# A cross-attention kernel on one core: moving casts, loads and evacuations between slots, and reordering its fill and its end

## The chip, the cores and the metric

The kernel runs on one core of a Trainium2 chip. The metric is the device time of one execution in microseconds (us), as the median of several runs. A core has a matrix engine (TensorE, PE in the profile; PEld is its weight load), a vector engine (VectorE, DVE), a scalar engine (ScalarE, ACT), a general engine (GpSimd, POOL) and a queue that only issues DMAs (SyncE, SP). Each engine works through its own instructions in program order, and waits on semaphores for the others. TensorE writes its products to PSUM; all else is in SBUF or in DRAM.

## The reference: what is computed

The inputs are x (32 batches of 512 rows of 640), a context (32 batches of 77 rows of 1024) and weights. All is float32.

```python
q = _heads(hidden_states @ to_q_w)                       # 20 heads of 32
h_txt = _sdpa(q, _heads(ehs_txt @ to_k_w), _heads(ehs_txt @ to_v_w))
...
out = out @ to_out_w + to_out_b
out = (out + residual) / RESCALE
```

`_sdpa` is softmax(q k^T / sqrt(32)) v. The context has exactly 77 rows, so the three other attentions of the reference work on empty slices, and their weights are not used. The output is attention, the output projection, its bias and x itself added.

## The kernel before

**Arithmetic.** Float32 operands are split in two float32r parts, a high part (a cast) and a low part (the source minus the high part), and a product is three matmuls: high by high, high by low, low by high (`PAIRS`, L127). So nearly every tile costs a cast, usually on ACT, and a subtraction on DVE or GpSimd.

**Order.** The order of the instructions of each engine is the program's (`manual_schedule`, L267): what the Python code calls first stands first on the engine, and DMAs on their queue. A tile pool hands out buffers (`bufs`), and a tile that takes a used buffer waits for the readers of the old one.

**First phase: keys and values.** Keys and values of all batches are computed in five groups of up to 512 context rows (L294 to L383), split (`split_keys` L207, `split_values` L222) and stored in DRAM (`k_dram`, `v_dram`). Query weights are loaded and split beside that, output weights too; these go to `wo_dram` (`split_wo`, L318). The values of the last group are left for the first slots of the next phase (`beside`).

**Second phase: slots.** A slot is one batch and one chunk of four heads: n = 5 b + j, 160 in all. "First" to "fifth slot" below are j = 0 to 4. In slot n (`slot`, L701) TensorE computes the scores of n in four blocks of 128 query rows (`scores` L464, each with a maximum per row on DVE, L486), the queries of slot n + 1 (`queries` L437), the product of probabilities and values of slot n - 4 (`values` L566), and a quarter of the output projection of an earlier batch (`piece` L637, matmuls L622). ACT computes exponentials (`exps` L491), GpSimd normalises (`normalize` L509), DVE transposes (`transpose_p` L517), and the probabilities go to DRAM (`pd`, SP) and come back transposed as a tile `raw` (`load_p` L533, two loads). There `cast_p` (L540) casts the last 64 rows (L544) and the rest (L545), `last_p` (GpSimd, L558) and `rest_p` (DVE, L551) make the low parts. `PASSES` (L564) gives the order in which the values' matmuls use them: first the cast, then the rows with `last_p`'s part, then `rest_p`'s.

After `values`, `copy_a` (ACT) and `add_a` (DVE) add the two halves; a slot later `high_a` (ACT, L599) and `low_a` (DVE, L604) make the operands of the output projection. `finish` (L648) evacuates closed projection banks with the residual added (DVE, L654) and stores them; there are two banks `po`. `split_q` (L451) copies the queries: ACT, two copies on GpSimd (L458), two subtractions on DVE (L460).

**Special slots.** A slot is "filling" when n > 0 and there is no finished batch to project yet (n = 1 to 7). In filling slots the big cast is GpSimd's. Values begin with slot 4 (`takes`, L665). `end` (L845) works off the last four slots' probabilities and the last projections.

**Queues.** SP issues nearly all DMAs: keys and values of a batch (`refill` L686), `pd` stores, `raw` loads, x, residuals, outputs. Each issue takes SP's time too, so what stands ahead on SP counts.

Lines that the steps below touch: L213, L234, L376, L544, L545, L551, L558, L599, L604, L654, L717 to L722, L754, L759, L783, L829 to L833, L845 to L887, L937 to L945.

## Time and profile before

| | us |
|---|---|
| median of 3 runs | 1945.45 (1943.25 to 1946.92) |
| the profiled execution's own time | 1956.04 |
| its span, first to last instruction | 1954.3 |
| PE, DVE, ACT, POOL busy | 1902.4, 1638.7, 1532.9, 1376.5 |
| first scores start (end of the first phase) | 265.0 |
| last scores' maximum (slot 159) | 1906.1 |

The profile is of one execution that is 10.6 us longer than the median run; sums made from its rows are made against 1956.04. A row of the timeline gives start, length, engine, line, operation, tiles and form; in brackets stand the engine's idle time before it and what ended that. A row of waits gives total, number of times and the longest. "x4" means that four instructions of one kind are drawn together. A matmul's busy time is modelled, since matmuls overlap; short waits inside a group show only as a longer group.

### The profile page before, as it was taken

The numbers are of one execution on the slowest core, as the hardware profiler recorded it, in microseconds if no ns is written. First come the engines' busy times: TensorE is split into PE (matmuls) and PEld (weight loads), VectorE is DVE, ScalarE is ACT, GpSimd is POOL, SyncE is SP. The second block draws the span as 40 slices with busy tenths as digits, with TensorE's granted clock in tenths as the row PEclk, the third lists the DMA queues.
The fourth block names the chain that finished last, engine by engine and source line by source line (L and its number), as shares of the span: only waits on it lengthen the run. The fifth ranks groups of instructions, "written<-read, shape, count | busy, mean of one in ns | idle before, by whom it ended". The sixth has DMA issues, their size and how long they took to land.

```text
span 1954.3 us, 37691 instructions
## 1 busy us (share of the span) xinstructions
PE 1902.4 (97%) x10332; PEld 1663.2 (85%) x10332; DVE 1638.7 (84%) x2494; ACT 1532.9 (78%) x6206; POOL 1376.5 (70%) x1264
## 2 busy tenths in 40 slices
PE   9999997999999999999999999999999999999998
PEld 7888886888888888888888888888888888888887
DVE  4444447899999989989999999999999999999995
ACT  3232247888899889888888888989988889889883
POOL 1000057888888888878888787888888888788874
PEclk9999998999999999999999999999999999999999
DMA  9878868898898988888888888988889898888875
GB/s 188 197 190 251 190 184 207 216 232 227 227 237 227 223 227 225 228 219 231 223 235 226 227 225 227 235 231 232 221 234 229 229 229 225 227 223 228 230 201 168
DMA packets 570657, 431.39 MB, mean 221 GB/s; under 512 B 199440, under 2 KB 479120, under 8 KB 570448
## 3 DMA queue, kind: packets, MB, share of 16 engines
q1 hardware_dynamic: 566832, 416.36, 84.6%
q0 software_dynamic: 3520, 12.45, 1.8%
q8 instruction: 86, 1.41, 0.3%
q14 instruction: 123, 1.01, 0.2%
q10 hardware_dynamic: 96, 0.16, 0.0%
HBM read 247.17 MB, written 181.64 MB: 219 GB/s over the span
## 4 chain that ended last, share of the span: by engine, by line
PE 43%; POOL 15%; DMA 13%; DVE 9%; ACT 7%; issue 7%; SPq 5%; POOLq 0%; DVEq 0%; ACTq 0%
PE po L622 11%; PE pq L443 11%; DMA raw<-pd 8%; PE pk L191 7%; PE pv L191 7%; POOL pn L513 5%; PE pa L573 4%; PE sc L478 4%; ACT pn L496 3%; POOL pp L558 3%; POOL qt L458 3%; POOL xt L264 2%; DMA xs<-in_x_dram 2%; DVE nm L486 2%; DVE pp L551 2%
## 5 line engine op out<-in xcount | busy, mean ns | idle before, releaser
L496 ACT ACTIVATE pn<-sc,nm 128x77 f32<-128x77 f32 x2560 | 794.3, 331 | 58.0 <-DVE nm L486 53.1
L622 PE MATMUL po<-wo_s,at 128*128 128x320 f32 x3840 | 629.1, 312 | 17.9 <-DVE xr L654 13.2
L443 PE MATMUL pq<-xt,wq_s 128*128 128x512 f32 x2400 | 631.5, 403 | 1.2
L622 PEld LDWEIGHTS po<-wo_s,at 128*128 128x128 f32 x3840 | 575.6, 188 | 47.8 <-DVE xr L654 26.5
L496 ACT ACTIVATION_READ_ACCUMULATOR pn<-sc,nm 128x1 f32 x2560 | 539.1, 211 | 0.0
L513 POOL TENSOR_TENSOR pn<-pn,rs 128x616 f32<-128x616 f32 x320 | 448.4, 1419 | 116.4 <-DVE rs L506 105.2
L443 PEld LDWEIGHTS pq<-xt,wq_s 128*128 128x128 f32 x2400 | 429.7, 191 | 85.8 <-POOL xt L264 10.8
L478 PEld LDWEIGHTS sc<-kb,qt 128*128 128x128 f32 x1920 | 327.2, 189 | 63.6 <-POOL qt L458 11.8
L478 PE MATMUL sc<-kb,qt 128*128 128x154 f32 (+1 forms) x1920 | 317.5, 273 | 16.4 <-POOL qt L458 7.7
L573 PE MATMUL pa<-pp,vb 128*128 128x512 f32 x960 | 295.7, 412 | 9.1 <-issue 5.1
L486 DVE TENSOR_REDUCE nm<-sc 128x4 f32<-128x308 f32 x640 | 285.6, 457 | 14.1 <-PE sc L478 9.3
L458 POOL CAST qt<-qt 64x512 fp32r<-64x512 f32 x320 | 194.9, 609 | 132.7 <-ACT qt L454 93.3
L551 DVE TENSOR_TENSOR pp<-raw,pp 128x1024 fp32r<-128x1024 f32 x160 | 272.3, 1702 | 14.2 <-ACT pp L545 11.9
L520 DVE STREAM_TRANSPOSE z<-pn 128x1280 f32<-128x1280 f32 x160 | 241.8, 1512 | 35.5 <-POOL pn L513 28.0
L558 POOL TENSOR_TENSOR pp<-raw,pp 64x512 fp32r<-64x512 f32 x160 | 207.0, 1294 | 56.8 <-ACT pp L544 44.6
L588 DVE TENSOR_TENSOR pa<-pa,aw 64x512 f32<-64x512 f32 x320 | 222.6, 696 | 14.6 <-ACT aw L583 4.1
L264 POOL TENSOR_TENSOR xt<-xs,xt 128x512 fp32r<-128x512 f32 x160 | 202.8, 1294 | 36.4 <-ACT xt L263 33.4
L460 DVE TENSOR_TENSOR qt<-pq,qt 64x512 fp32r<-64x512 f32 x320 | 218.6, 683 | 10.0 <-ACT qt L454 5.0
L615 POOL TENSOR_TENSOR xr<-xr,bias 128x640 f32<-128x640 f32 x128 | 203.2, 1588 | 12.4 <-PE sc L478 3.0
L573 PEld LDWEIGHTS pa<-pp,vb 128*128 128x128 f32 x960 | 160.3, 190 | 46.5 <-POOL pp L558 15.8
L544 ACT CAST pp<-raw 64x512 fp32r<-64x512 f32 x160 | 99.2, 620 | 101.2 <-DMA raw<-pd 97.4
L583 ACT COPY aw<-pa 64x1024 f32<-64x1024 f32 x160 | 162.0, 1013 | 19.2 <-PE pa L573 15.5
(47 smaller groups left out, 1656.5 us busy)
## 6 DMA issues: line engine op xcount, KB each, us to landing
pd<-z SPq DMA_DIRECT2D x640, 160.0 KB, 3.4
raw<-pd SPq DMA_DIRECT2D x160, 512.0 KB, 4.4
xr<-in_x_dram SPq DMA_DIRECT2D x128, 320.0 KB, 3.8
out_dram<-xr SPq DMA_DIRECT2D x127, 320.0 KB, 3.7
xs<-in_x_dram SPq DMA_DIRECT2D x124, 320.0 KB, 7.2
raw<-pd SPq DMA_DIRECT2D x160, 128.0 KB, 4.4
v_dram<-vs SPq DMA_DIRECT2D x80, 192.0 KB, 4.0
k_dram<-ks POOLq DMA_DIRECT2D x20, 512.0 KB, 4.7
```

Source lines behind the costliest of these rows:

```text
L191: nc.tensor.matmul(held[j][:, :gn], w[:, k, a, :], cts[g, k][:, c, :gn], start=(k == 0 and n == 0), stop=(k == NK - 1 and n == 2),)
L264: low.tensor_tensor(parts[1], src, parts[0].bitcast(F32), ALU.subtract)
L443: nc.tensor.matmul(pqs[n], wq_s[:, k, a, j * P : (j + 1) * P], xts[b, k][:, c, :], start=(k == 0 and m == 0), stop=(k == NC_ - 1 and m == 2),)
L458: nc.gpsimd.tensor_copy(qt[other, 1 + w, :], qt[r, 0, :].bitcast(F32))
L478: nc.tensor.matmul(sc[:, cols], qt[:, m, t * P : (t + 1) * P], keys_, start=(m == 0), stop=(m == 2),)
L486: nc.vector.tensor_reduce(nm, sc[:, :KCOLS].rearrange("p (h k) -> p h k", k=NKEY), AX.X, ALU.max, negate=True)
L496: nc.scalar.activation(pnb[n % 2][:, at, :NKEY], sc[:, i * NKEY : (i + 1) * NKEY], AF.Exp, bias=nm[:, i : i + 1], accum_out=sms[n][:, at : ...
L513: nc.gpsimd.tensor_tensor(pf, pf, rs[:, k : k + half].unsqueeze(2).to_broadcast([P, half, NKEY]), ALU.mult)
L551: nc.vector.tensor_tensor(pp[:, 2:4, :], raw[:, 0:2, :], pp[:, 0:2, :].bitcast(F32), ALU.subtract)
L558: nc.gpsimd.tensor_tensor(pp[64:, 4, :], raw[:64, 2, :], pp[:64, 4, :].bitcast(F32), ALU.subtract)
L573: nc.tensor.matmul(pas[n][:, p, :], vb[:, p, t, :], pp[:, c, :], start=(c == p), stop=(c == p + 2),)
L622: nc.tensor.matmul(pos[b, t, h][:, :HALF], ats[b * NC_ + j][:, a, t * P : (t + 1) * P], wos[0][:, j, c, h * HALF : (h + 1) * HALF], start= ...
```

## The change

It does these things.

- **Fourth slot.** `cast_p` is parted: `cast_rows` casts the last 64 rows. Third slots cast the rows of the tile that the fourth slot takes, before their last exponentials. From the fourth slot on (j >= 3) `high_a` goes before the big cast; so far only j = 4 did that.
- **Loads of probabilities** go at the top of the slot in third slots and in filling slots (`soon`), instead of after the second scores.
- **Fifth slot.** `finish()` is called before the last scores too.
- **Filling slots.** The big cast comes after the second exponentials, `rest_p` before and `last_p` and the key copies after `split_q`. Exponentials of the fourth block go ahead of `copy_a` and x splits, and of the value splits beside.
- **Output weights** are loaded once, into the tiles of z, the second value tile and the bias before these are needed, and split in slots 1, 2 and 5. `wo_dram` goes.
- **Values beside** (last group, chunks 2 to 4): the low part and the four stores move from DVE and SP to GpSimd.
- **First slot.** The last group's last two key stores are issued by ACT. Both key loads, the output weights and x of batch 1 follow on SP; x of batch 1 was on GpSimd's queue. The second value tile is zeroed in slot 3.
- **End.** The load for slot 158 moves ahead of the residual, the eight value loads and the last transpose; one `finish()` goes.

TensorE's order of matmuls is the same in both.

```diff
-    wo_dram = dram.tile([P, NC_, 2, C], FPR, name="wo_dram")
...
-    def split(hi, lo, src):
+    def split(hi, lo, src, low=nc.vector):
         nc.scalar.copy(hi, src)
-        nc.vector.tensor_tensor(lo, src, hi.bitcast(F32), ALU.subtract)
+        low.tensor_tensor(lo, src, hi.bitcast(F32), ALU.subtract)
...
         split(ks[:, 0, :gn], ks[:, 1, :gn], pks.pop(j)[:, :gn])
-        engine = nc.gpsimd if g + 1 < len(GROUPS_KV) else nc.sync
+        engine = nc.gpsimd if g + 1 < len(GROUPS_KV) else nc.sync if j < 3 else nc.scalar
         j0 = GROUPS[GROUP_OF[j]][0]
...
-    def split_values(g, j, between=None):
+    def split_values(g, j, between=None, low=nc.vector):
...
             between()
-        split(vs[:, :na, 0], vs[:, :na, 2], vt)
+        split(vs[:, :na, 0], vs[:, :na, 2], vt, low)
+        queue = nc.sync if low is nc.vector else low
         dst = v_dram[g0 : g0 + gn, :, j].rearrange("(a t) i c d -> i t a (c d)", t=Q)
         for i in range(HPC):
-            nc.sync.dma_start(
+            queue.dma_start(
                 dst[i].bitcast(F32),
...
         nc.gpsimd.tensor_copy(kb[64:, 3], kb[64:, 2].bitcast(F32))
+
+    def zero_values(g):
+        vbs[g] = main.tile([P, GROUPS[g][1], 2, 2, P], FPR, tag=f"vb{g}", name=f"vb{g}")
+        nc.gpsimd.memset(vbs[g].bitcast(F32), 0.0)
...
+    def cast_rows(n):
+        pps[n] = late[0].tile([P, 5, S], FPR, tag="pp", name="pp", bufs=1)
+        nc.scalar.copy(pps[n][:64, 4, :], raws[n][:64, 2, :])
+
     def cast_p(n, shared=False):
...
         raw = raws[n]
-        pp = late[0].tile([P, 5, S], FPR, tag="pp", name="pp", bufs=1)
-        nc.scalar.copy(pp[:64, 4, :], raw[:64, 2, :])
-        (nc.gpsimd.tensor_copy if shared else nc.scalar.copy)(pp[:, 0:2, :], raw[:, 0:2, :])
-        pps[n] = pp
+        if n not in pps:
+            cast_rows(n)
+        (nc.gpsimd.tensor_copy if shared else nc.scalar.copy)(pps[n][:, 0:2, :], raw[:, 0:2, :])
...
-        raw, pp = raws.pop(n), pps[n]
+        raw, pp = raws[n], pps[n]
         nc.vector.tensor_tensor(
...
-    WO = {1: (0, 1, 2), 5: (3,), 6: (4,)}
+    WO = {1: (0, 1), 2: (2, 3), 5: (4,)}
     wos = []
+    wo_raw = {}
+
+    def load_wo(tag, *ks):
+        rows = wo.rearrange("(c p) n -> p c n", p=P)
+        raw = main.tile([P, len(ks), C], F32, tag=tag, name="wo_raw")
+        for i, k in enumerate(ks):
+            nc.sync.dma_start(raw[:, i], rows[:, k])
+            wo_raw[k] = raw[:, i]
+
+    def split_wo(k):
+        split(wos[0][:, k, 0], wos[0][:, k, 1], wo_raw[k])
...
                 load_x(b + 1, (3,))
-            load_keys(b, 1, heads)
+            if b:
+                load_keys(b, 1, heads)
         elif j == 1 and b:
...
         filling = n > 0 and not has_out
+        soon = n >= LATE and (filling or j == 2)
+        if soon:
+            load_p(n - LAG + 1)
         if not filling:
...
             copied = None
-        if taken is not None and j != NC_ - 1:
-            cast_p(taken, filling)
+        if taken is not None and not filling and j < 3:
+            cast_p(taken)
         if n - 1 in takes:
             high_a(takes[n - 1])
-        if taken is not None and j == NC_ - 1:
-            cast_p(taken, filling)
+        if taken is not None and not filling and j >= 3:
+            cast_p(taken)
         bias_now = j in BIAS and b >= BIAS[j][0]
...
             normalize(n - 1, rss.pop(n - 1))
-        if taken is not None:
+        if taken is not None and not filling:
             last_p(taken)
-        if copied is not None:
+        if copied is not None and not (filling and taken is not None):
             copy_keys(copied)
...
             low_a(takes[n - 1])
-        if taken is not None:
+        if taken is not None and not filling:
             rest_p(taken)
-        if n == LATE + 2:
-            nc.sync.dma_start(bias, bo.unsqueeze(0).to_broadcast([P, C]))
-        if n >= LATE:
+        if n == LATE + 3:
+            biases.append(main.tile([P, C], F32, tag="bias", name="bias"))
+            nc.sync.dma_start(biases[0], bo.unsqueeze(0).to_broadcast([P, C]))
+        if n >= LATE and not soon:
             load_p(n - LAG + 1)
...
             refill(b, j, 0)
-        for k in WO.get(n, ()):
-            nc.sync.dma_start(wos[0][:, k].bitcast(F32), wo_dram[:, k].bitcast(F32))
         refill(b, j, 1)
...
         exps(n, 1, *s)
+        if taken is not None and filling:
+            cast_p(taken, True)
+        for k in WO.get(n, ()):
+            split_wo(k)
+        if n == 3:
+            load_wo("bias", 4)
+            zero_values(1)
         for i in turns[0]:
...
                 values(taken, 0, 4)
+                finish()
                 s3 = scores(n, 3)
...
         if ahead:
+            if taken is not None and filling:
+                rest_p(taken)
             split_q(n + 1)
+            if taken is not None and filling:
+                last_p(taken)
+                if copied is not None:
+                    copy_keys(copied)
             if parted:
...
                 values(taken)
-        if len(beside) > 0:
-            context_values(LAST, beside[0], psv)
+        for c in beside:
+            values_of(LAST, c, psv)
         finish()
...
             transpose_x(b + 1, i)
-        if taken is not None:
+        if has_out:
             copy_a(taken)
-        for c in xsplits[1]:
-            split_x(b + 1, c)
+            for c in xsplits[1]:
+                split_x(b + 1, c)
+            if j == 2:
+                cast_rows(takes[n + 1])
         exps(n, 3, *s)
+        for c in beside:
+            split_values(LAST, c, low=nc.gpsimd)
+        if not has_out:
+            if taken is not None:
+                copy_a(taken)
+            for c in xsplits[1]:
+                split_x(b + 1, c)
         if has_out and j in (4, 0, 1):
...
             add_a(taken)
-        if len(beside) > 1:
-            context_values(LAST, beside[1], psv)
         if has_out:
...
         load_p(N - 3)
-        load_values(last, 1)
-        load_residual(last - 1, 3)
         piece(last - 1, 4)
...
         rest_p(N - 4)
+        load_p(N - 2)
+        load_residual(last - 1, 3)
+        load_values(last, 1)
         transpose_p(N - 1)
         add_bias(last - 1, 2)
-        load_p(N - 2)
         piece(last - 1, 5)
...
         steps(last - 1, 32, 37)
-        finish()
         values(N - 3)
...
     load_keys(0, 0)
+    load_keys(0, 1)
+    load_wo("z", 0, 1)
+    load_wo("vb1", 2)
+    load_wo("bias", 3)
+    load_x(1)
     queries(0, 0, NC_)
...
     copy_keys(0)
-    for vb in vbs:
-        nc.gpsimd.memset(vb.bitcast(F32), 0.0)
+    zero_values(0)
     context_values(LAST, 0, psv)
```

The hunks left out drop the loads and splits of the output weights from the first phase, and arguments that nothing uses any more.

More of the change, by code (lines that the diff above doesn't have):

```diff
@@ L99, with load_weights @@
     v_dram = dram.tile([NT + KPAD - NKEY, HPC, NC_, 3, HD], FPR, name="v_dram")
-    wo_dram = dram.tile([P, NC_, 2, C], FPR, name="wo_dram")
-    def split(hi, lo, src):
+    def split(hi, lo, src, low=nc.vector):
         nc.scalar.copy(hi, src)
-        nc.vector.tensor_tensor(lo, src, hi.bitcast(F32), ALU.subtract)
-    def load_weights(w, k0, kn, permuted=True, queues=(nc.sync,) * 4, tag="wraw"):
+        low.tensor_tensor(lo, src, hi.bitcast(F32), ALU.subtract)
+    def load_weights(w, k0, kn, queues=(nc.sync,) * 4, tag="wraw"):
         raw = kvw.tile([P, 2, C], F32, tag=tag, name="wraw", bufs=3 if tag == "wraw" else 2)
-        if permuted:
-            rows = w.rearrange("(q c i) n -> q i c n", q=4, i=Q)
-            for q, queue in enumerate(queues):
-                queue.dma_start(raw[q * Q : (q + 1) * Q, :kn], rows[q, :, k0 : k0 + kn])
-        else:
-            rows = w.rearrange("(c p) n -> p c n", p=P)
-            nc.sync.dma_start(raw[:, :kn], rows[:, k0 : k0 + kn])
+        rows = w.rearrange("(q c i) n -> q i c n", q=4, i=Q)
+        for q, queue in enumerate(queues):
+            queue.dma_start(raw[q * Q : (q + 1) * Q, :kn], rows[q, :, k0 : k0 + kn])
         for k in range(kn):
@@ L243, with load_x @@
     xts, xss, xpool = {}, {}, []
-    def load_x(b, quarters=range(4), queue=nc.sync):
+    def load_x(b, quarters=range(4)):
         if b not in xss:
@@ L251, in load_x @@
         for q in quarters:
-            queue.dma_start(xs[q * Q : (q + 1) * Q, :, :], src[q])
+            nc.sync.dma_start(xs[q * Q : (q + 1) * Q, :, :], src[q])
     def transpose_x(b, i):
@@ L316, in split_wq @@
         split_weights(wq_s[:, k], wq, k, scale=SCALE)
-    def split_wo():
-        k = len(split_ks) - NC_
-        split_ks.append(k)
-        ws = kvw.tile([P, 2, C], FPR, tag="ws", name="ws", bufs=2)
-        split_weights(ws, wo, k)
-        nc.sync.dma_start(wo_dram[:, k].bitcast(F32), ws.bitcast(F32))
     load_context(1, NK)
@@ L348 @@
                     split_keys(0, 4)
-                split_values(g, 3, (None, split_wq, split_wo, None)[g])
+                split_values(g, 3, (None, split_wq, None, None)[g])
                 context(g + 1, *range(3, NK))
@@ L359 @@
                     load_x(0)
-            split_values(g, j, (None, split_wq, split_wo, None)[g])
+            split_values(g, j, (None, split_wq, None, None)[g])
         if g + 1 < LAST:
             load_context(g + 2, NK)
-            if g < 2:
+            if not g:
                 for k in range(0, NC_, 2):
-                    load_weights((wq, wo)[g], k, min(2, NC_ - k), permuted=g == 0)
+                    load_weights(wq, k, min(2, NC_ - k))
             for k in range(NK):
@@ L375 @@
         split_x(0, c)
-    load_x(1, queue=nc.gpsimd)
     for round_ in (range(3), range(3, NC_)):
@@ L393 @@
     raws, pps, ats, pds, sms, pqs, pas, xrs, pos, aws, rss = ({} for _ in range(11))
-    bias = main.tile([P, C], F32, name="bias")
+    biases, zs = [], []
     kbs, vbs, pnb = [], [], []
@@ L405 @@
     qts = [main.tile([P, 3, S], FPR, name=f"qt{n}") for n in range(2)]
-    z = main.tile([P, NBLK, NQ, Q], F32, name="z")
     for g, (j0, nj) in enumerate(GROUPS):
-        vb = main.tile([P, nj, 2, 2, P], FPR, name=f"vb{g}")
-        vbs.append(vb)
+        vbs.append(None)
     def load_keys(b, g, heads=range(HPC)):
@@ L517, in transpose_p @@
     def transpose_p(n):
-        pn = pnb[n % 2]
+        if not zs:
+            zs.append(main.tile([P, NBLK, NQ, Q], F32, tag="z", name="z"))
+        z, pn = zs[0], pnb[n % 2]
         nc.vector.transpose(
@@ L614, in add_bias @@
     def add_bias(b, t):
-        nc.gpsimd.tensor_tensor(xrs[b, t], xrs[b, t], bias, ALU.add)
+        nc.gpsimd.tensor_tensor(xrs[b, t], xrs[b, t], biases[0], ALU.add)
     def output_bank(b, t, h):
```

## The prediction

> **What bounds the kernel now.** I read the page's busy shares and slices first, then stretches of the span, then the waits, then the timeline of one batch.
>
> ```profile
> PE 1902.4 (97%) x10332; PEld 1663.2 (85%) x10332; DVE 1638.7 (84%) x2494; ACT 1532.9 (78%) x6206; POOL 1376.5 (70%) x1264
> ...
> PE   9999997999999999999999999999999999999998
> ```
>
> TensorE (PE) is busy in every slice but the seventh and the last, so at most the 52 us that it idles can go, plus waits too short to show as gaps. The stretches show where they are (PE busy is the first figure behind the length, PEclk the granted clock, then the DMA engines' share):
>
> ```profile
> 318.00:350.00 32.00, 25.04 (x105) 19.83 (x104) 27.30 (x42) 23.17 (x103) 23.82 (x22) 0.87 1.00 234
> ...
> 361.00:1898.00 1537.00, 1515.37 (x8541) 1334.05 (x8540) 1418.86 (x2155) 1366.22 (x5692) 1250.88 (x1136) 1.00 0.88 227
> ...
> 1926.00:1930.00 4.00, 0.00 (x0) 0.00 (x0) 0.71 (x2) 2.15 (x3) 1.26 (x1) 1.00 0.91 265
> ...
> 316.00:319.40 3.40, 3.19 (x8) 2.50 (x9) 2.70 (x5) 0.77 (x2) 1.63 (x3) 0.50 1.16 219
> ```
>
> Three places: the steady part (361 to 1898), where PE lacks 22 us in 30 batches; the fill (about 262 to 361), where PE stalls and its clock drops to half for stretches of 3.4 us; the end, where it stands 4 us. A batch of five slots takes 51.3 us on average in the steady part (from each first-slot reduce L486 to the next) and 50.46 at best.
>
> In a fifth slot (n = 64) the timeline shows the steady loss that comes every time:
>
> ```profile
> 929.19 1.28 POOL L558 TENSOR_TENSOR pp<-raw,pp 64x512 fp32r<-64x512 f32 x1
> 929.39 2.16 DVE L551 TENSOR_TENSOR pp<-raw,pp 128x1024 fp32r<-128x1024 f32 x1 [0.38 <-ACT pp L545]
> ...
> 930.55 2.09 POOL L513 TENSOR_TENSOR pn<-pn,rs 128x616 f32<-128x616 f32 x1
> ...
> 931.48 0.85 DVE L486 TENSOR_REDUCE nm<-sc 128x4 f32<-128x308 f32 x2
> ...
> 932.25 0.87 DVE L654 TENSOR_TENSOR xr<-po,xr 128x320 f32<-128x320 f32 x2
> ...
> 932.78 2.90 PE L622 MATMUL po<-wo_s,at 128*128 128x320 f32 x18 [0.44 <-DVE xr L654]
> ```
>
> PE's 18 projection matmuls wait for the first evacuation L654 (932.25 to 932.73), which stands behind two reduces. In the slot before it (n = 63), ACT is the late one:
>
> ```profile
> 917.24 0.62 ACT L544 CAST pp<-raw 64x512 fp32r<-64x512 f32 x1
> ...
> 917.99 1.29 POOL L558 TENSOR_TENSOR pp<-raw,pp 64x512 fp32r<-64x512 f32 x1 [0.38 <-ACT pp L544]
> ...
> 918.71 0.57 ACT L599 CAST at<-pa 128x512 fp32r<-128x512 f32 x1
> ...
> 919.32 0.69 DVE L604 TENSOR_TENSOR at<-pa,at 128x512 fp32r<-128x512 f32 x1 [0.77 <-ACT at L599]
> ```
>
> and the waits of 425 to 1860 (28 batches) say how much this is:
>
> ```profile
> ACT pp L544 <- DMA raw<-pd: 73.5, 70, 3.2
> ...
> POOL pp L558 <- ACT pp L544: 23.4, 25, 1.9
> ```
>
> **Steady part, fifth slots.** finish() now stands before the last scores. TensorE's order is unchanged; on DVE both evacuations pass one reduce. The first then starts after one reduce of 0.43 (0.85 for two) instead of two and PE gets its bank 0.4 us earlier. The reduce behind it comes 0.8 later; its exponentials started only at 934.56, behind copy_a, 2.2 us after the reduce, which hides it. Thirty fifth slots (n = 9 to 154): 12 us. Ends: nothing (if the next late thing, the query copies on GpSimd up to 933.98 and DVE's up to 934.45, were to be PE's next wait; PE comes at 935.5 now, 935.1 then) and 0.6 a slot with the weight loads' wait (24.8 us for 30).
>
> **Steady part, fourth slots.** The third slot takes the rows' cast (0.62) before its last exponentials; the fourth slot's ACT then starts with high_a and only then the big cast (1.05). ACT's sum is unchanged. In the slot shown, GpSimd's L558 could start when GpSimd is free at 917.61 (0.3 to 0.4 earlier) and DVE's L604 about 0.7 earlier. From L558 on GpSimd runs nearly without a gap through L513, the query copies, the x splits and key copies into the fifth slot's L558 (930.47), for which PE's values wait: what GpSimd gains it hands to PE. Over the window it waited 23.4 us for that cast, and nearly all of it lies in fourth slots, where the load lands late. The load (issued 912.22 and 912.65 behind four loads of values) now goes first in the third slot, at about 908.8. It would land about 913.7, from 4.5 us of the shown one, 2 us before ACT wants it. The four value loads move back 0.9 us and are wanted a slot and a half later. Of 23.4 for 28 batches I take 23 for 30 (third slots from n = 12); ends are 0.3 a batch (9, the floor of the shown slot) and 25.
>
> Together 35. From this I take back a third, 12 us: of the 73.5 us that ACT waits for raw tiles most lies in second and third slots, whose loads don't move in the loop. It is harmless today as PE runs ahead of ACT; with batches about a microsecond shorter and DMA engines at 0.88 already, part of it will reach PE. Net steady: **-23** (ends -8 and -36).
>
> A rule weighs on this. The Trainium skill (SBUF — State Buffer, section Who interferes with whom) says that a DVE operation with two SBUF inputs and a GpSimd operation reading SBUF exclude each other for a whole instruction. The rows agree: L551 took 2.16 beside L558 and ended 1.08 after it, and takes 1.20 elsewhere; L513 took 2.09 against 1.23. By the rule, the L551 of the fourth slot gains GpSimd's 0.3 and not ACT's 0.6, which would make the gain of the fourth slots 9 instead of 23, and the net some 9 us smaller.
>
> **Fill.** Removed: five splits and stores of the output weights in the key and value phase, where PE has no gap, so worth nothing. The round trip through DRAM (1.6 MB each way) goes, which the DMA engines (share 1.00 from 318 to 350) feel. Gains: the first scores waited 2.3 us (262.7 to 265.0) for key copies, held by five stores behind each other on SP and the load of x beside them; three stores now stand before the keys. In filling slots the query copies go ahead of L558 and the key copies, and raw loads go first. TensorE's gaps there for query copies are 7.7 us in 8, and each long one halves the clock for 3.4 us (six matmuls L443 took 2.76 instead of 1.60, so about 1.2 us).
> Costs: GpSimd takes three value splits (1.29 for 512 columns, so about 1.05 for 416) and twelve stores at 0.66 (its four x loads took 2.61), plus a 0.95 memset later: 12 us on GpSimd between about 272 and 305, where it was busy half the time. They stand before normalisations and the fifth slot's query copies, which I get 3 to 4 us late. The first two value stores wait on SP behind 2.6 MB of loads, and the third chunk's transpose waits for the first. The output weights' five splits cost ACT 0.73 and DVE 0.8 each. I get slots 0 to 4 about even, or 4 us worse, and slots 5 to 7 (318 to 350) 2 to 4 us better, since DVE's 27.3 of 32 us doesn't shrink. Sum **-1** (ends -10, all of the query gaps and the first wait with no new one, and +6).
>
> The same skill (TensorE: Matmul & The Clock Gate, What's actually happening) puts the half clock behind an idle window of about 3.4 us. The row of 316 shows 0.50 after a gap of 2.7; by the page only the end's gap would cost clock, and the fill's better end would be -6 instead of -10, three drops of 1.2 less.
>
> **End.** The 4.3 us gap (1925.8 to 1930.1) is ACT waiting for the raw tile of slot 158, issued at 1921.4 behind eight value loads (5.2 us), a residual and a pd store. It now goes before all these, at about 1913.3, when L551 has freed its buffer, and lands near 1919. Slot 159's tile is then next: its pd store follows the value loads, about 1.3 us later than today, so it lands near 1932 and PE waits about 2 us for it, where it waits 0.2 now. The dropped finish() decouples DVE from a bias add, 0.1 us. With the half clock that followed the gap saved in part: **-3.5** (ends -1 and -6).
>
> **Sum.** -23 - 1 - 3.5 = -27.5. The profiled execution took 1956.0 (span 1954.3), so 1928.5 in its terms. The median shown is 10.6 lower, 1945.5, so **1918**.
>
> **Rivals.** (1) Raw tiles bound it: DMA engines at 0.88 give back all of the fourth slots; 12 less a third stays, and the end: 1945 - 8 - 3.5, about 1934. For it: 73.5 us of waits, DMA share 1.00 in the fill. Against: the best batches, without such waits, still take 50.46.
> (2) All goes, fill and end too: -36 - 10 - 6 gives 1893. For it: PE's own work in a batch. Against: DVE is busy 1419 of 1537 us.
> (3) Slower: the rows' cast waits for its raw tile in the third slot, now with four exponentials and the fourth slot's normalisation behind it. It decides from the point where the tile lands over 7.1 us after its issue (908.8 to 915.9); landing 9.5 us after it costs 2.4 a batch, of which PE's lead covers perhaps 1, so 1.4 by 30 = 42, less 12 and 3.5: 1972. For it: tiles beside x loads took 6.8 (928.5 to 935.3). Against: x loads are not in flight in third slots.
> (4) The finish() does nothing, as L551 is the real releaser, and the rest cancels: about 1945.
>
> **How the numbers follow.** Forecast 0.56 (1905 to 1930), rival 1 0.20 (1930 to 1941), rival 2 0.12 (under 1905), rival 4 0.04, rival 3 0.08. A measurement of this kernel tells about 0.2% (3.9 us). Faster is the first three, 0.88; same 0.04; slower 0.08. Range 1898 to 1939: the forecast, rival 1 nearly whole and the upper part of rival 2.
>
> **What would show it.** Right: the wait of L622 for L654 falls from 24.8 to under 8; L558's wait for ACT from 23.4 to under 4; batches near 50.4; no 4 us gap near the end. Wrong: a growing wait of ACT L544-type casts on raw tiles, in third slots above all; scores waiting for GpSimd's query copies by over 3 us around slot 4.

## The result, and the profile after

| | before | after |
|---|---|---|
| median of 4 runs, same chip, us | 1944.35 (1940.36 to 1946.92) | 1960.78 (1958.18 to 1971.10) |
| profiled execution's own time (span) | 1956.04 (1954.3) | 1971.10 (1969.3) |
| slot 0 starts, slot 10 starts | 266.0, 372.6 | 263.2, 388.2 |
| slot 10 to slot 155 | 1488.4 | 1488.7 |
| start of slot 159 to the end | 54.0 | 53.9 |

The ratio is 1.010, with a 95% interval of 1.0064 to 1.0137: the change made the kernel 12 to 27 us slower, where 27 us faster was forecast. A slot starts here with its first maximum (L486, L476 after). The table says where to look: slot 10 is 15.6 us late, and what follows took as long as before. The busy shares and slices of the changed kernel's page:

```profile
PE 1911.5 (97%) x10332; PEld 1668.7 (85%) x10332; DVE 1633.9 (83%) x2491; ACT 1529.3 (78%) x6206; POOL 1391.9 (71%) x1275
...
PE   9999987899999999999999999999999999999998
...
PEclk9999997899999999999999999999999999999999
```

PE's row had one weak slice, the seventh, and has three, the sixth to the eighth; the clock falls in two of them. PE is busy 9 us more with the same number of matmuls; the mean granted clock of the execution fell from 0.993 to 0.987, so they take longer. The stretches of the changed kernel, with the columns of those shown of before (the first and third are those of the fill and the steady part there; the second is one stretch after a PE gap; the last is the gap near the end):

```profile
318.00:350.00 32.00, 21.98 (x82) 17.00 (x82) 22.16 (x32) 19.52 (x91) 20.45 (x21) 0.81 0.75 167
335.50:338.50 3.00, 3.00 (x9) 2.52 (x10) 1.49 (x1) 2.17 (x9) 0.00 (x0) 0.50 0.19 39
361.00:1898.00 1537.00, 1519.06 (x8522) 1334.36 (x8523) 1413.32 (x2150) 1361.20 (x5675) 1259.52 (x1139) 1.00 0.89 226
1946.50:1950.00 3.50, 0.10 (x2) 0.04 (x1) 0.85 (x2) 2.15 (x3) 2.28 (x2) 0.83 0.82 310
```

In 318 to 350 PE is busy 22.0 us instead of 25.0, and the DMA share is 0.75 where it was 1.00: full DMA engines are not what holds this stretch now. PE's rows of the timeline that carry a wait show what:

```profile
311.40 0.49 PE L468 MATMUL sc<-kb,qt 128*128 128x154 f32 x1 [5.37 <-POOL qt L448]
...
323.17 1.34 PE L568 MATMUL pa<-pp,vb 128*128 128x512 f32 x4 [3.21 <-POOL pp L553]
335.47 2.08 PE L568 MATMUL pa<-pp,vb 128*128 128x512 f32 x4 [3.61 <-POOL pp L553]
347.94 2.06 PE L568 MATMUL pa<-pp,vb 128*128 128x512 f32 x4 [2.99 <-POOL pp L553]
...
361.12 2.08 PE L568 MATMUL pa<-pp,vb 128*128 128x512 f32 x4 [2.99 <-POOL pp L553]
```

The first row is the query copies for slot 4, for which PE waited 0.40 us before and waits 5.37 now. On GpSimd the moved value work stands ahead of them:

```profile
302.20 1.08 POOL L103 TENSOR_TENSOR vs<-vs 128x416 fp32r<-128x416 f32 x1 [1.20 <-ACT vs L102]
303.58 2.58 POOL L230 DMA_DIRECT2D v_dram<-vs  x4 [0.30 <-POOL vs L103]
...
307.39 2.40 POOL L503 TENSOR_TENSOR pn<-pn,rs 128x616 f32<-128x616 f32 x2
...
310.75 1.27 POOL L448 CAST qt<-qt 64x512 fp32r<-64x512 f32 x2
```

In each slot from 4 to 7 the values' third to sixth matmuls wait some 3 us for `last_p` (L553, L558 before), which now stands behind the query copies on GpSimd. An earlier gap of 5.30 us (275.4 to 280.7) comes from DVE, where the transpose of a value chunk stands in front of slot 0's work until a store has landed. Below, the first row is DVE's, the second SP's (eight value stores, behind output weights and x):

```profile
277.40 0.62 DVE L223 STREAM_TRANSPOSE vs<-pv 128x416 f32<-128x416 f32 x1 [8.68 <-DMA v_dram<-vs]
```

```profile
266.83 9.61 SPq L230 DMA_DIRECT2D v_dram<-vs  x8
```

The steady part did change inside. The fourth and the fifth slot that were shown of before (n = 63 and 64) are now:

```profile
930.53 1.28 POOL L553 TENSOR_TENSOR pp<-raw,pp 64x512 fp32r<-64x512 f32 x1
...
930.75 0.59 ACT L594 CAST at<-pa 128x512 fp32r<-128x512 f32 x1
...
931.51 0.67 DVE L599 TENSOR_TENSOR at<-pa,at 128x512 fp32r<-128x512 f32 x1
...
944.02 0.47 DVE L476 TENSOR_REDUCE nm<-sc 128x4 f32<-128x308 f32 x1
...
944.41 0.87 DVE L649 TENSOR_TENSOR xr<-po,xr 128x320 f32<-128x320 f32 x2
...
944.94 1.73 PE L617 MATMUL po<-wo_s,at 128*128 128x320 f32 x10
```

GpSimd and DVE wait for no cast of ACT, and one reduce instead of two stands before the evacuations, as forecast. The waits of 425 to 1860:

```profile
ACT pp L534 <- DMA raw<-pd: 91.2, 61, 4.4
...
POOL pp L553 <- ACT pp L534: 14.9, 19, 2.3
...
PEld po L617 <- DVE xr L649: 14.5, 33, 0.5
```

GpSimd waits 14.9 us for ACT instead of 23.4, and PE's weight loads 14.5 for the evacuation (24.8 before, in the same window), but ACT waits 91.2 for raw tiles instead of 73.5.

To see what reaches PE I use its **excess**: the time from each matmul's start to the next one's, above the lower quartile for that pair of lines and shapes, summed over 28 batches (good to 1 or 2 us). By slot of the batch, first to fifth, it was 6.7, 8.7, 8.5, 17.3, 48.3 us before and is 6.9, 25.2, 13.0, 9.3, 37.1 after. Fourth and fifth slots gained 19 us; second and third gave 21 back.

### The profile page after: what moved, and what is told of

It is laid out like the page before. It is cut to its first block, busy times and chain, and to the rows that moved or that the text cites. A ratio compares the mean times of both kernels' runs of the same rounds, so it can differ in the third digit from the quotient of the medians.

```text
span 1969.3 us, 37733 instructions
## 1 busy us (share of the span) xinstructions
PE 1911.5 (97%) x10332; PEld 1668.7 (85%) x10332; DVE 1633.9 (83%) x2491; ACT 1529.3 (78%) x6206; POOL 1391.9 (71%) x1275
## 3 DMA queue, kind: packets, MB, share of 16 engines
HBM read 243.89 MB, written 178.36 MB: 214 GB/s over the span
## 4 chain that ended last, share of the span: by engine, by line
PE 28%; DMA 22%; ACT 19%; POOL 10%; DVE 8%; issue 6%; SPq 6%; POOLq 0%; DVEq 0%; ACTq 0%
DMA raw<-pd 10%; ACT pn L486 10%; PE pk L186 7%; PE pv L186 6%; PE po L617 6%; PE pq L433 5%; DMA xs<-in_x_dram 5%; DMA pd<-z 4%; POOL pn L503 3%; PE pa L568 3%; PE sc L468 2%; POOL qt L448 2%; SPq L519 2%; POOL pp L553 2%; ACT aw L578 2%
## 5 line engine op out<-in xcount | busy, mean ns | idle before, releaser
L486 ACT ACTIVATE pn<-sc,nm 128x77 f32<-128x77 f32 x2560 | 795.3, 335 | 64.4 <-DVE nm L476 58.2
L617 PEld LDWEIGHTS po<-wo_s,at 128*128 128x128 f32 x3840 | 576.4, 189 | 28.8 <-DVE xr L649 14.9
L486 ACT ACTIVATION_READ_ACCUMULATOR pn<-sc,nm 128x1 f32 x2560 | 550.0, 215 | 0.0
L503 POOL TENSOR_TENSOR pn<-pn,rs 128x616 f32<-128x616 f32 x320 | 457.6, 1447 | 118.0 <-DVE rs L496 104.8
L568 PE MATMUL pa<-pp,vb 128*128 128x512 f32 x960 | 302.0, 420 | 33.4 <-POOL pp L553 13.9
L476 DVE TENSOR_REDUCE nm<-sc 128x4 f32<-128x308 f32 x640 | 287.9, 457 | 19.2 <-PE sc L468 12.5
L448 POOL CAST qt<-qt 64x512 fp32r<-64x512 f32 x320 | 199.0, 622 | 142.9 <-ACT qt L444 114.1
L546 DVE TENSOR_TENSOR pp<-raw,pp 128x1024 fp32r<-128x1024 f32 x160 | 265.9, 1662 | 20.5 <-ACT pp L541 11.9
L553 POOL TENSOR_TENSOR pp<-raw,pp 64x512 fp32r<-64x512 f32 x160 | 206.2, 1289 | 43.6 <-ACT pp L534 27.9
L610 POOL TENSOR_TENSOR xr<-xr,bias 128x640 f32<-128x640 f32 x128 | 202.7, 1585 | 11.7 <-DMA vb<-v_dram 2.1
```

Of the source, the lines that this page charges most:

```text
L448: nc.gpsimd.tensor_copy(qt[other, 1 + w, :], qt[r, 0, :].bitcast(F32))
L476: nc.vector.tensor_reduce(nm, sc[:, :KCOLS].rearrange("p (h k) -> p h k", k=NKEY), AX.X, ALU.max, negate=True)
L486: nc.scalar.activation(pnb[n % 2][:, at, :NKEY], sc[:, i * NKEY : (i + 1) * NKEY], AF.Exp, bias=nm[:, i : i + 1], accum_out=sms[n][:, at : ...
L503: nc.gpsimd.tensor_tensor(pf, pf, rs[:, k : k + half].unsqueeze(2).to_broadcast([P, half, NKEY]), ALU.mult)
L546: nc.vector.tensor_tensor(pp[:, 2:4, :], raw[:, 0:2, :], pp[:, 0:2, :].bitcast(F32), ALU.subtract)
L553: nc.gpsimd.tensor_tensor(pp[64:, 4, :], raw[:64, 2, :], pp[:64, 4, :].bitcast(F32), ALU.subtract)
```

## The experiments

The kernel before took 1944 us on the chip of the first comparison and 1949 to 1953 on those of the experiments, so ratios to the runs of before on the same chip are compared. Slot 10 and the stretch from slot 10 to slot 155 are of one profiled execution each.

| run | ratio to before (95%) | slot 10 | 10 to 155 | 159 to end |
|---|---|---|---|---|
| e5 changed kernel again | 1.0075 (1.0059 to 1.0092) | 388.3 | 1479.4 | 53.3 |
| e6 kernel before again | 0.9998 (0.9985 to 1.0011) | 372.4 | 1484.5 | 54.9 |
| e1 steady part and end | 0.9933 (0.9911 to 0.9955) | 371.0 | 1476.4 | 54.1 |
| e11 finish() alone | 0.9994 (0.9980 to 1.0009) | 370.8 | 1481.3 | 54.6 |
| e12 fourth slot alone | 0.9951 (0.9931 to 0.9972) | 370.5 | 1478.1 | 55.4 |
| e2 both, load between | 0.9949 (0.9931 to 0.9967) | 372.8 | 1471.9 | 55.7 |
| e7 e2 and another end | 0.9929 (0.9913 to 0.9945) | 369.5 | 1474.3 | 49.2 |
| e9 changed, load between | 1.0093 (1.0072 to 1.0114) | 389.4 | 1484.5 | 52.2 |
| e3 changed, filling order of before | 1.0016 (1.0003 to 1.0030) | 379.7 | 1481.2 | 53.5 |
| e15 of this, `last_p` and its like alone | 1.0028 (1.0014 to 1.0043) | 380.5 | 1481.4 | 55.5 |
| e16 of this, `copy_a` alone | 1.0071 (1.0049 to 1.0093) | 386.6 | 1479.1 | 54.2 |
| e4 changed, values stored first | 1.0067 (1.0049 to 1.0084) | 390.2 | 1479.8 | 54.1 |
| e8 e4 and x early | 1.0048 (1.0031 to 1.0065) | 384.9 | 1481.7 | 54.1 |
| e10 changed, repaired | 0.9974 (0.9960 to 0.9988) | 373.6 | 1484.0 | 49.5 |
| e13 e10 and a spacer in DRAM | 0.9927 (0.9913 to 0.9941) | 373.4 | 1472.3 | 51.7 |
| e14 changed, spacer alone | 1.0038 (1.0023 to 1.0052) | 388.7 | 1474.4 | 54.2 |
| e17 e13, values on DVE | 0.9943 (0.9925 to 0.9961) | 374.4 | 1471.6 | 50.0 |
| e18 e7 and a spacer | 0.9974 (0.9960 to 0.9989) | 369.2 | 1483.8 | 50.6 |

**Both kernels again (e5, e6; no edit).**

> The changed kernel once more, beside the kernel before and the others of this call on one chip. In the first profile the stretch from slot 10 to slot 155 took 1488.7 us, as before; two kernels with the same steady code took 1481 and 1480 there. Theory 'the first profile's steady part fell on late tiles': 1478 to 1484 here, and the whole is slower than before by the fill's 15.6 less 5 to 8, about 0.5%. Rival 'steady gains nothing': 1488 again, and slower by 0.8 to 1%.

> The kernel before, as a kernel of its own: what the comparison itself leaves open. Ratio 1.000, within 0.002; slot 10 to 155 in 1486 to 1490 us if that stretch repeats itself, slot 10 at 372 to 373.

Before against itself gives 1.000. The fill repeats itself (slot 10 at 388.3 and 372.4); the steady stretch doesn't, it spreads by 4 us before and 9 us after. The first profile's steady part was a late one, as the first theory had it, and the ratio 1.0075 is nearer to its rival's.

**Steady part and end alone (e1):** the kernel before with the two diffs below (e11's and e12's) and the change's `end`.

> The kernel before with the changes of the third, fourth and fifth slots of the steady part and of the end; first slot, filling slots, output weights and values beside as before. Theory 'fill' (all of the loss comes from the filling slots, and the steady part and the end lose nothing and gain nothing, since SP may not issue a DMA before the eighth one ahead of it has landed and the third slot's early load makes it wait 1.4 us a batch): 1944, within 4. Rival 'carried over' (the steady part would have gained what was forecast, if the fill had not left it late): about 1918. Rival 'steady loses too': over 1950.

Neither extreme: 13 us gained (9 to 17), so the steady part does bring something. Its halves, `finish()` (e11) and the fourth slot (e12):

```diff
                 values(taken, 0, 4)
+                finish()
                 s3 = scores(n, 3)
```

```diff
+        if has_out and j == 2: load_p(n - LAG + 1)
         if not filling: refill(b, j, 0)
-        if taken is not None and j != NC_ - 1: cast_p(taken, filling)
+        if taken is not None and (filling or j < 3): cast_p(taken, filling)
         if n - 1 in takes: high_a(takes[n - 1])
-        if taken is not None and j == NC_ - 1: cast_p(taken, filling)
+        if taken is not None and not filling and j >= 3: cast_p(taken, filling)
...
+        if has_out and j == 2: cast_rows(takes[n + 1])
         exps(n, 3, *s)
```

> The kernel before with finish() ahead of the last scores of the fifth slot, and nothing else. Forecast of the prediction: 12 us. From the runs with all the changes TensorE's excess in fifth slots fell from 48 to 37 us in 28 batches: if that is finish() alone and nothing gives it back, slots 10 to 155 take 1474 to 1478 us (before: 1488 and 1485), ratio 0.994. Rival 'given back by the tiles': 1480 to 1484, ratio 0.997 to 0.999, with more excess in second and fourth slots.

> The kernel before with the fourth slot's change alone: rows cast in the third slot, high_a first from the fourth slot on, third slot's load ahead of all eight value loads. Forecast of the prediction: 23 us, of which a part is given back. From the runs with all the changes TensorE's excess in fourth slots fell from 17 (15) to 9 us and second slots rose from 8 to 12 to 25. Theory 'eight in flight': gain and loss nearly cancel, slots 10 to 155 take 1482 to 1488 us, ratio 0.998 to 1.001. Rival 'the forecast gain is there by itself': 1470, ratio 0.992.

`finish()` alone: the excess between the values and L622 in fifth slots fell from 16.9 to 6.0 us, by 11 where 12 were forecast, and fifth slots as a whole from 49.0 (e6) to 40.1. But fourth slots rose by 2.7, second and third by 1.3 and 1.1, and of the whole 1.2 us are left (3.9 faster to 1.8 slower). The fourth slot alone: its own excess fell from 15.4 to 7.6, fifth slots from 49.0 to 42.7, and second slots rose from 8.3 to 14.0; 9.6 us are left (5.5 to 13.5). So "gain and loss nearly cancel" is refuted too, and the size forecast as well.

**Eight DMAs in flight (e2, e9).** In both traces no DMA that SP issues starts before the eighth one ahead of it has landed (2551 and 2533 pairs, the nearest some 16 ns after). With the third slot's load ahead of eight value loads, the last of them wait for it. SP's waits in the steady part of e5, and below of e9, where one edit puts the load between the value loads (rows: total, times, longest):

```profile
SPq L422 <- DMA raw<-pd: 39.8, 31, 2.1
...
SPq L519 <- DMA raw<-pd: 27.0, 59, 1.4
```

```profile
SPq L519 <- DMA raw<-pd: 24.8, 54, 1.1
```

```diff
-        soon = n >= LATE and (filling or j == 2)
+        soon = n >= LATE and filling
...
             refill(b, j, 0)
+        if has_out and j == 2:
+            soon = True
+            load_p(n - LAG + 1)
```

> The kernel before with the changes of the third, fourth and fifth slots only (end and fill as before), but the third slot's load of probabilities stands behind its first four value loads instead of ahead of them. Theory 'eight in flight': the 8th DMA behind that load is then one of the pd stores and not the last value loads, so SP does not stand before these; the rows' cast of second slots waits about 35 us again instead of 59, TensorE's excess in second slots falls from 25 us to about 9, and the fourth and fifth slots keep their gain of some 19 us: about 1927 (1920 to 1932). Rival 'DMA engines are full' (the order among loads does not matter, a tile that is earlier makes another later): second slots stay 25 us over, and the time is 1940 to 1946.

> The changed kernel with one edit: the third slot's load stands behind its first four value loads instead of ahead of them. Theory 'eight in flight': SP's waits for the eighth DMA ahead fall from 112 us in the whole execution to about 50, the rows' cast of second slots waits less, and slots 10 to 155 take 1473 us as in the two kernels with that order and the fill of before, instead of 1479 to 1482: some 7 us, ratio 1.004 where the changed kernel had 1.0075. Rival 'the fill's disorder or the other addresses of its tiles' (what makes the steady part of the changed kernel 3 to 5 us worse than with the fill of before): 1477 or more.

The value loads' waits are gone, and the time isn't: e9 against e5 1.0093 to 1.0075, e2 against e1 0.9949 to 0.9933. The theory fell. Something else came back: with the load later, the rows' cast in third slots waits for its tile (8.4 us over 28 batches in e9, none in e5), and PE's weight loads of the scores wait 16.1 us for ACT's exponentials instead of 2.8 (425 to 1860); the excess of fourth slots rises by some 7 us. But e2 and e9 have the same steady code, and differ by 12.6 us in it (1471.9, 1484.5): something outside the steady code matters.

**The place of the probabilities in DRAM (e13, e14, e18).** Without `wo_dram` the DRAM tiles `pd`, which are allocated after it, move down by its 3.28 MB. A spacer puts them back; e10 (below) is the repaired kernel without it.

```diff
+    space = dram.tile([P, NC_, 2, C], FPR, name="space")
...
         split_weights(wq_s[:, k], wq, k, scale=SCALE)
+        if not k:
+            nc.sync.dma_start(space[:1, 0].bitcast(F32), wq_s[:1, 0].bitcast(F32))
```

> The repaired kernel with one thing more: a DRAM tile of the size of wo_dram (128 x 5 x 2 x 640 floats, 3.28 MB), of which one row is written once, so that the probabilities' DRAM tiles (pd) lie where they lay before the change. Theory 'place of pd': without wo_dram these tiles moved down by its size, and their loads land 0.2 us later than in the kernels with wo_dram (median 4.49 us against 4.07 and 4.13 where the order of the steady part is the same). Then the median goes back to 4.1, slots 10 to 155 take 1472 to 1476 us instead of 1484, ratio 0.992 to 0.994. Rival 'carried over from the fill, or places in SBUF': 4.4 to 4.5 and 1481 to 1486, ratio 0.997 as without the spacer.

> The changed kernel with the same spacer in DRAM and nothing else. Theory 'place of pd': median landing of raw tiles 4.4 instead of 4.7, slots 10 to 155 in 1474 to 1477 us as with the fill of before instead of 1479 to 1482, ratio 1.004 to 1.006 instead of 1.0075. Rival: 1479 or more, ratio 1.007 or more.

> The kernel before with the changes of third to fifth slots, load between, new end (0.9929, raw tiles landing after 4.1 us, slots 10 to 155 in 1474 us), and the spacer: the probabilities' DRAM tiles lie 3.28 MB above the place of before, where the changed kernel had them 3.28 MB below it. If the changed kernel's place is a bad one and most are alike: nothing changes (0.992 to 0.994, 4.1 us). If the place of before is a good one and others are worse: landing 4.4 to 4.5, 1481 to 1485, ratio 0.996 to 0.998.

The DMA issues of e10 and of e13 (the last figure is the median from issue to landing, us), and their steady stretches:

```profile
raw<-pd SPq DMA_DIRECT2D x160, 512.0 KB, 4.5
```

```profile
raw<-pd SPq DMA_DIRECT2D x160, 512.0 KB, 4.1
```

```profile
373.60:1857.60 1484.00, 1471.90 (x8269) 1288.80 (x8268) 1366.18 (x2090) 1321.92 (x5510) 1215.83 (x1103) 1.00 0.89 228
```

```profile
373.40:1845.70 1472.30, 1466.13 (x8269) 1288.13 (x8268) 1362.57 (x2090) 1323.93 (x5510) 1219.09 (x1103) 1.00 0.88 230
```

Same code, same fill (slot 10 at 373.6 and 373.4), and 11.7 us less. In ratios the place is worth 0.0047 between e10 and e13, 0.0037 between e5 and e14, 0.0045 between e7 and e18: 7 to 9 us each. The spacer's own small store is not the cause, since the same edit made e13 faster and e18 slower. The runs of each pair were on different chips, but one chip shows it too: with the same steady code e17 and e18 have landings of 4.0 and 4.4 and steady stretches of 1471.6 and 1483.8 on one chip, and on another e14 has 1474.4 where e3, e4, e15 and e16 have 1479.1 to 1481.4. In e14 the time came as its theory had it, the landing less clearly: the page's median for the 512 KB loads is 4.7 (4.8 in e5), for the 128 KB loads 4.2 (4.8). That the time goes by the landings is thus likely, not shown. The third place, 3.28 MB above that of before, is as slow as that of e10 (landing 4.4): the kernel before had the good one of three.

**The fill: filling order (e3, e15, e16).** Of the two edits below, e15 makes the first, e16 the second, e3 both; the comment stands for the calls that go back to their old places:

```diff
-            split_q(n + 1)
-            if taken is not None and filling: last_p(taken); copy_keys(copied)
+            # cast_p at the slot's top, last_p after scores 0, rest_p after scores 1
+            split_q(n + 1)
...
+        if taken is not None: copy_a(taken)
         exps(n, 3, *s)
-        if not has_out: copy_a(taken)
```

> The changed kernel, but filling slots work in the order of before: big cast, the rows' subtraction and key copies at the start of the slot, the rest's subtraction after the second scores, copy_a ahead of the last exponentials. Theory 'closed loop' (the rows' subtraction behind the query copies makes TensorE's values wait 3 us in each of slots 4 to 7, and copy_a behind the exponentials makes the next normalisation late): these four stalls go, some of the old waits for query copies come back, slot 10 starts about 8 us earlier, 1953 (1949 to 1956). Rival 'GpSimd' (its value stores make the slots late, whatever the order): 1960, within 3.

> The changed kernel with the filling slots' big cast, rows' subtraction, rest's subtraction and key copies where they were, copy_a still behind the last exponentials. Together with copy_a both gave 8.5 us. Theory 'rows' subtraction behind the query copies' makes most of it: TensorE's waits of 3 us for GpSimd's rows in slots 4 to 7 go, slot 10 at 380 to 382. Rival 'copy_a behind the exponentials' makes most: slot 10 at 385 to 388.

> The changed kernel with copy_a and the x splits ahead of the last exponentials in the filling slots again, the rest of the new filling order kept. Theory 'rows' subtraction': the waits of 3 us for GpSimd's rows stay, slot 10 at 386 to 388. Rival 'copy_a': slot 10 at 380 to 383.

The order of the casts and subtractions makes 7.8 of 8.6 us, `copy_a` alone 1.7. PE's waits in e15, where the values' waits of 3 us are gone and shorter ones for query copies are back:

```profile
312.69 0.50 PE L468 MATMUL sc<-kb,qt 128*128 128x154 f32 x1 [5.37 <-POOL qt L448]
...
324.97 0.34 PE L468 MATMUL sc<-kb,qt 128*128 128x154 f32 x1 [2.40 <-POOL qt L448]
...
344.03 0.34 PE L468 MATMUL sc<-kb,qt 128*128 128x154 f32 x1 [1.50 <-POOL qt L448]
...
361.45 0.73 PE L568 MATMUL pa<-pp,vb 128*128 128x512 f32 x2 [0.23 <-POOL pp L553]
```

**The fill: slot 0 (e4, e8).** e4 moves the loads of output weights and x of batch 1 behind the first chunk's `context_values`; e8 does this and loads x of batch 1 on GpSimd's queue where it was before.

```diff
-    load_wo("z", 0, 1); load_wo("vb1", 2); load_wo("bias", 3); load_x(1)
     queries(0, 0, NC_)
...
     context_values(LAST, 0, psv)
+    load_wo("z", 0, 1); load_wo("vb1", 2); load_wo("bias", 3); load_x(1)     # e8: load_x(1, queue=nc.gpsimd), before
```

> The changed kernel, but SP issues the value stores of the last group's first chunk before the loads of output weights and of x of batch 1. Theory 'store behind loads' (DVE's transpose of the third chunk waited 8.7 us until these stores had landed at 277, and with it the maxima and exponentials of slot 0, so TensorE stood 5.3 us at 275.4): the gap goes, slot 2 starts some 4 us earlier, and 2 to 4 us of it are left at slot 10: about 1957. Rival: the chain on GpSimd from 278 on holds slots 2 to 4 where they are: 1960, within 2.

> The changed kernel, but x of batch 1 is loaded on GpSimd's queue where it was before, and SP issues the value stores of the last group's first chunk ahead of the output weights. Storing the values first alone had moved the wait: the transpose of x stood in front of DVE's queue until x landed at 280.5, and TensorE stood 6.7 us. Theory 'two late things' (value store and x, either of which holds DVE): the 5.3 us gap goes, slot 2 starts 4 to 5 us earlier than in the changed kernel, and slot 10 some 4 us earlier: 0.2% better than the changed kernel. Rival 'GpSimd holds the next slots anyway': slot 4 and later start as in the changed kernel, within 1 us.

e4 was a miss: slot 2 came at 292.3 instead of 290.0. The value transpose no longer waits, but x is later on SP, its transpose is next on DVE, and waits 7.91 us for x; the gap is 6.68. With both edits PE has no gap over 0.9 there and slot 10 comes 3.4 us earlier. Two late things stood behind each other, and curing one shows the other.

**All repairs, and what is left (e10, e17).** e10 has e3, e8, e9's load and e7's end. e17 gives the values' low parts and stores back to DVE and SP (`split_values(LAST, c)`), with the spacer.

> The changed kernel with all the repairs that were tried one by one: x of batch 1 early on GpSimd's queue and the first values stored ahead of the output weights (-3.4 us at slot 10), the filling order of before (-8.5), the third slot's load between the value loads (-7 in the steady part), the value loads of the end behind the last pd stores (-5). If they add up: slot 10 at 376 to 377, steady part 1473 to 1476, end 49 to 50, ratio 0.995 to 0.997. If the rest of the fill's loss (GpSimd's value stores) grows when the others go: slot 10 at 380 or more, ratio 0.998 or more.

> The repaired kernel with the spacer in DRAM, and the low parts and stores of the values beside on DVE and SP again, as before the change. Theory 'GpSimd's stores': from slot 0 to slot 4 the repaired kernels take 43 us and the kernel before 39, since each of three chunks costs GpSimd a subtraction of 1.06 and four stores of 0.66 ahead of normalisations and query copies; 3 to 4 us of it go, slot 4 starts at 303 to 304 and slot 10 at 369 to 371: ratio 0.990 to 0.991. Rival (output weights split in slots 1 and 2 and their loads hold these slots): slot 4 at 306 or later, ratio 0.992 to 0.994.

Slot 10 came at 373.6, even better than the sum; the steady part at 1484 was not repaired by the load's place, which led to the spacer. In e17 PE's wait for query copies at slot 4 fell from 4.7 to 0.7, as the theory had it, but slots 0 to 2 took 35.0 us instead of 32.9, slot 4 came at 306.8 as the rival had it, and slot 10 gained nothing. The theory is right about this wait and wrong in the sum. The splits of output weights in slots 1 and 2 were not tried by themselves.

**The end (e7).** In the changed kernel's end SP's rows show the value loads in front of the last pd stores, and PE's row the price:

```profile
1928.34 0.37 SPq L528 DMA_DIRECT2D raw<-pd  x1
...
1929.97 6.06 SPq L422 DMA_DIRECT2D vb<-v_dram  x8
1936.14 2.35 SPq L519 DMA_DIRECT2D pd<-z  x4
```

```profile
1949.99 0.76 PE L568 MATMUL pa<-pp,vb 128*128 128x512 f32 x1 [3.40 <-DVE at L599]
```

e7 is e2 with the changed kernel's end, in which one line moves:

```diff
         load_residual(last - 1, 3)
-        load_values(last, 1)
         transpose_p(N - 1)
+        load_values(last, 1)
```

> The kernel before with the changes of the third, fourth and fifth slots, the third slot's load behind its first four value loads, and a new end: as in the change the load for slot 158 goes ahead of residual and value loads, but the eight value loads go behind the last transpose's pd stores. Theory 'pd stores behind value loads' (the change's end gained nothing since the pd stores of slot 159 stood behind eight value loads of 6.1 us, so that TensorE waited 3.4 us for that tile): both gaps of 3 to 4 us go, the end takes 50 us from slot 159 instead of 54, and with the steady part's 12 to 16 the whole is 0.8 to 1% faster than before. Rival: the value loads are now late themselves and the gap moves to the values of slot 158: end 53 to 54, whole 0.5 to 0.7% faster.

The end took 49.2 us, and after the first 2 us no gap of PE in it is over 0.53. e7 and e13 are 0.7% faster than before (intervals 0.55 to 0.87% and 0.59 to 0.87%), faster than both kernels.

## Why the prediction was wrong

| term | forecast, us | measured |
|---|---|---|
| fill | -1 (-10 to +6) | +15.6 and +15.9 at slot 10 |
| steady, fifth slots | -12 | -1.2 alone (e11) |
| steady, fourth slots | -23 | -9.6 alone (e12) |
| steady, net | -23 (-8 to -36) | -10 with the load between (e2), -13 with the end (e1) |
| place of `pd` | not there | +7 to +9 (e14, e13, e18) |
| end | -3.5 (-1 to -6) | 0 to -1.6 in the traces |

The forecast was 27.5 us faster. Fill +16, steady part and end -13 (e1, which has the changed kernel's order there) and place +7 to +9 make +10 to +12; the ratios of the two comparisons are +15 us (e5: 12 to 18) and +19 (12 to 27). What is missing is within e1's interval (9 to 17 us).

- **The fill failed, at "slots 0 to 4 about even, or 4 us worse, and slots 5 to 7 2 to 4 better".** Slots 0 to 4 took 63.7 us instead of 52.1, slots 5 to 7 39.1 instead of 31.9. The first scores did come earlier, by 2.8 us. GpSimd's 12 us of new work were sized rightly, and slot 4's query copies, forecast 3 to 4 us late, cost PE 5.37 us instead of 0.40: the sign of being wrong that the prediction named. That this work is the cause of that wait e17 shows (0.7), though there other waits took its place. Then, for slots 5 to 7, I counted the waits that the new order removes (PE for these slots' query copies, which went down as forecast) and not that `last_p`, put behind these copies, is itself what PE's values wait for: e15 gives 7.8 us of it back. For slot 0 I named the value stores behind 2.6 MB of loads, but priced them inside "4 us worse"; the stretch showed a 5.3 us gap with half a clock behind it, and x behind that (e8: 3.4 us).
- **The fourth slots were over-sized.** The 23.4 us that GpSimd waited for ACT were handed to PE one to one, though PE's excess in fourth slots was only 17.3. And PE's excess doesn't follow that wait: in e12, with 13.2 us of it left, the excess fell by 8 in fourth and by 6 in fifth slots, of which second slots took 6 back; in e7, with 4.0 left, fourth slots' excess fell by less than 1. In the changed kernel 14.9 are left, where the prediction's sign was under 4; the evacuation's 14.5 are not under 8 either. In the changed kernel DVE's subtraction L551 of the fourth slots starts 0.95 us earlier (1.76 instead of 2.71 after the slot's start) but takes 2.05 instead of 1.75 (means of 28).
- The Trainium skill's page SBUF — State Buffer (Who interferes with whom), weighed in the prediction, would have made the net some 9 us smaller, about -14. By e2 and e1 that is the nearer sum. The longer subtraction in the changed kernel's fourth slots agrees, e7's (1.64) doesn't; no run took the two engines' operations apart.
- **The third taken back for raw tiles** had the right mechanism and place in second slots (25.2 and 16.3 us of excess in the two profiles of the changed kernel). In the old place of `pd` it was there too while the load stood first (e12: 14.0 against 8.3), and smaller with the load between (e2: 11.3).
- **The place of `pd` was in no term and no rival.** It goes with later raw tiles, as in rival 1, but comes from an edit that I priced at nothing: the round trip of the output weights that goes. (That is 3.28 MB each way, not 1.6: the page's bytes read fall from 247.17 to 243.89 MB, those written from 181.64 to 178.36.)
- **The end:** the gap for slot 158 went (4.30 to 0.06), as forecast. "About 1.3 us later" for slot 159's pd stores was 2.7 (eight value loads of 6.06 instead of 5.20), and "about 2 us" of wait was 3.40, with half a clock behind it. e7's end shows that the order, not the idea, was at fault.
- **Rivals.** Rival 3, the only slower one, isn't what happened: the rows' cast in the changed kernel's third slots waits 0.14 us in 28 batches. With the load between it does wait (8.1 us in e7, 8.4 in e9). Rival 4's premise (L654 isn't the releaser) is refuted by e11's 11 us at that wait, though the whole stayed where it said.
- **Sums.** 24.8 us over 30 slots are 0.83 each, not 0.6, and the ends -8 and -36 of the net are not what the ends of its terms add up to (9 and 43 before anything is taken back).

## What to carry to other kernels

When an instruction is moved behind others on its engine, price who waits for the moved one as well as who is freed; in this fill, where little runs ahead, 7.8 us of such waits reached slot 10. A wait of an engine off the path is not yet a gain (23.4 us here, of which PE got 8); the excess of the engine that sets the end, in that same slot (17.3), is a closer bound. Where an edit removes or adds a DRAM tile, test the place of the others by a spacer before explaining small steady differences by the order of instructions.

## What the runs showed of the hardware that I had not expected

- The same 512 KB loads land after 4.1 or 4.5 us (medians, e13 and e10) by where their source tiles lie in DRAM, with an unused tile of 3.28 MB ahead of them as the only edit; the 2048-byte packets of these loads took 110 and 114 ns in the mean. Two of three places were slow. Why is open: no run measured places by themselves. The Trainium skill's page DMA: Bandwidth & Descriptors (Latency and other measured facts) knows a rate that depends on a row pitch of large powers of two; here the pitch is the same in both, so it does not settle this.
- In stretches of 3.0 to 3.4 us after PE gaps the clock was 0.50 or 0.51 for gaps of 2.99, 3.40, 3.61 and 5.30 us (changed kernel), 0.63 for 3.21, 0.67 for 2.40 (e15), and 1.00 for 1.12, 1.50 and 1.65 (e15): the drop does not grow evenly with the gap. The Trainium skill's page TensorE: Matmul & The Clock Gate (What's actually happening) gives an idle window of about 3.4 us; here 2.99 was enough, and 2.7 in the prediction's row.
